# Requests for rows and weights, and steps of the last routing, placed between the outputs behind attention

## The chip, the cores and the metric

The kernel runs on one core of one Trainium2 chip. The metric is the device time of one execution in microseconds (us). The engines are named as in the profile: PE is TensorE (matrix products; PEld its weight loads), DVE is VectorE, ACT is ScalarE, POOL is GpSimd, SP is SyncE, which here only issues transfers.

## The reference

Two gated layers are applied to `x` of 4 sequences of 512 tokens with 256 features, in float32. Only the end of the second layer matters here, the feed-forward part with four experts:

```python
x = x + tanh(g_xattn[1]) * attention(layernorm(x), ctx)      # 16 heads, softmax
h = layernorm(x).reshape(-1, 256)
expert = argmax(h @ W_router, axis=-1)                       # one of 4 for each token
a = gelu(h @ W1[expert] + b1[expert])                        # 1024 wide, erf form
y = a @ Wo + bo + h
x = x + tanh(g_ffn[1]) * layer_norm(y, gamma, beta)
```

The reference computes all four experts for every token and keeps one.

## The kernel before

**Tiles by expert.** The kernel computes for each token only its own expert. Tokens are sorted into tiles of 128 of one expert each; 19 tiles (`T_ALL = 16 + 3`) are enough whatever the split. The lists are made in three goes (`LISTS`, `dispatch`): after two sequences tiles 0 to 4 are known, after three sequences tiles 5 to 8, and after the last sequence tiles 9 to 18. The last list needs the routing of the last sequence (`route(3)`), and that needs the last output of attention.

**What one tile needs.** `fetch_rows(j)` (L950) gathers 128 rows of 512 floats (the normed row, and the row to add the result to) by an indirect transfer from the scratch tensor `rows_d`, into a buffer `xr` (5 of them) or `xg`. `fetch_weights(j)` (L962) gathers the tile's first weight matrix with its bias, 128 x 2056 floats, into `wg`. Both are issued by POOL, on one queue with everything else that POOL does. `turn_tile(j)`, called t below, transposes the normed rows on PE (L974) and copies them on ACT (DVE for j = 4) to `xs` (L977). `hidden_half(j, f2)`, two of which make h, is 32 matrix products (L996) followed by GELU on ACT (L1009; for tiles 0 to 3 the GELU is deferred, since attention holds ACT's table). `output_tile(j)`, called o, is an addition on DVE (L1175), 16 matrix products `pyf` (L1178) and another addition on DVE (L1182). `norm_tile(j)` is the layer norm of the result: on DVE statistics (L1187, L1189) and variance (L1192), on POOL one power of -0.5 (L1193), and on DVE the rest (L1194, L1195 to L1200). L1194 doesn't need the power; L1195 does. `put_tile(j)` (L1205) writes the finished rows to the output by an indirect transfer that POOL issues; each such write waits for the one before it.

**The last routing.** `route(3)` consists of steps: `stats3` and `more3` (L325 to L340: layer norm statistics on DVE, power and correction on POOL), `norm3` (L360, L721: normed rows on DVE, then two writes to `rows_d` by SP, L725 and L726), `turn3` (8 transposes on PE, L371; the two halves of `xTf` are copied by ACT and by DVE, L372), `products3` (16 products `plT` with the router's weights on PE, L738, and a copy on ACT, L743), `logits3` (a transpose on PE, L748, and five small DVE steps, L751 to L756, that mark each token's expert in `onehot`), `ranks3` (two products `prk` on PE, L764, and sums on DVE, L767, L768). Then `dispatch(2)`: `lists`, `token_places` and `by_tile` (small DVE steps, L812 to L879; POOL clears one buffer, L872), `sels` (four selections of 128 x 512 on DVE, L899), `by_expert` (L886 to L892), `collected` (32 products `pidT` on PE, L912, and a copy on ACT, L917) and `tokens` (a transpose on PE, L921, and four small DVE steps, L923 to L930, that write the indices which `fetch_rows(9)` and later ones read).

**Order.** From here on no scheduler decides: each engine executes its instructions in the order in which the program emits them (`manual_schedule`). Behind the last attention group the program emits a block with all requests for tiles 5 to 8, into which the last routing's norm is put after the rows of tile 3, and then walks a list of items `queue`. For each item the loop emits the item; for an output it emits norm and put with it; then it emits the steps of the last routing that are assigned to this item (`steps`), and requests for later tiles. The order before is:

h4, o0, o1, o2, t5, o3, h5, t6, o4, h6, t7, o5, h7, t8, o6, h8, o7, t9, o8, h9, t10, h10, t11, o9, h11, and from there t, o, h for each tile.

The steps are assigned like this:

```python
    steps = {
        ("o", 1): [turn3], ("o", 2): [products3], ("o", 3): [logits3],
        ("h", 5): [ranks3, lists, token_places, by_tile], ("o", 4): [*sels, by_expert],
        ("o", 5): [collected], ("h", 7): [tokens],
    }
```

Requests for tiles 9 and 10 follow output 6, those for 11 follow output 7, and from output 8 on each output j is followed by those for tile j + 4. [...]

Of the kernel before, what the change touches and what calls it, by code (L numbers as in the profile page):

```python
# [20 lines left out]
B, S, D = 4, 512, 256  # L21
# [27 lines left out]
def flamingo_kernel(ctx: ExitStack, tc: tile.TileContext, t: dict, out: bass.AP):  # L49
    nc = tc.nc  # L50
# [654 lines left out]
    def route(b, eng=None):  # L705

        st = {}

        def stats():
            st["xn"] = act.tile([P, NT, D], F32, tag="xn", name=f"xn_f1_{b}")  # L710
            first, st["more"], st["rows"] = layernorm(
                x[b], st["xn"], 1e-5, f"f1_{b}", eng
            )
            first()

        def more_stats():
            st["more"]()

        def norm():
            st["rows"]()  # L720
            (eng or nc.gpsimd).tensor_tensor(  # L721
                x[b], x[b], bet1.unsqueeze(1).to_broadcast([P, NT, D]), ALU.add
            )
            rd = rows_d[b * S : (b + 1) * S, :].rearrange("(n p) d -> p n d", p=P)
            nc.sync.dma_start(out=rd[:, :, 0:D], in_=st["xn"])  # L725
            nc.sync.dma_start(out=rd[:, :, D : 2 * D], in_=x[b])  # L726

        def turn():
            st["xT"] = act.tile([P, NC, S], F32, tag="blocks", name=f"xTf1_{b}", bufs=1)
            transposed(st["xn"], st["xT"], f"f1_{b}")  # L730

        def products():


            plT = bank_psum(f"plT{b}")[:, 0:P]
            for c in range(NC):
                for n in range(NT):
                    nc.tensor.matmul(  # L738
                        plT[n * HP : (n + 1) * HP, :], lhsT=wr[:, c, :], rhs=st["xT"][:, c, ts(n, P)],
                        start=(c == 0), stop=(c == NC - 1),  # L740
                    )
            st["lT"] = const.tile([P, P], F32, tag="dec", name=f"lT{b}")
            nc.scalar.copy(st["lT"], plT)  # L743

        def logits():

            plg = bank_psum(f"plg{b}")[:, 0:P]
            nc.tensor.transpose(plg, st["lT"], ident)  # L748
            plg = plg.rearrange("p (n e) -> p n e", e=HP)[:, :, 0:NE]
            top = sml.tile([P, NT], F32, tag="top", name=f"top{b}")  # L750
            nc.vector.tensor_reduce(top, plg, AX.X, ALU.max)  # L751
            oh = onehot[:, ts(b, NT), :]
            nc.vector.tensor_tensor(oh, plg, top.unsqueeze(2).to_broadcast([P, NT, NE]), ALU.is_ge)
            nc.vector.tensor_tensor(oh, oh, order, ALU.mult)
            nc.vector.tensor_reduce(top, oh, AX.X, ALU.max)
            nc.vector.tensor_tensor(oh, oh, top.unsqueeze(2).to_broadcast([P, NT, NE]), ALU.is_equal)  # L756

        def ranks():
            prk = bank_psum(f"prk{b}")[:, 0 : 2 * NT * NE].rearrange(
                "p (i n e) -> p i n e", i=2, e=NE  # L760
            )
            oh = onehot[:, ts(b, NT), :]
            for i, m in enumerate((before, ones)):
                nc.tensor.matmul(prk[:, i], lhsT=m, rhs=oh, start=True, stop=True)  # L764
            for n in range(NT):
                k = b * NT + n
                nc.vector.tensor_tensor(count[:, k + 1, :], count[:, k, :], prk[:, 1, n, :], ALU.add)  # L767
            nc.vector.tensor_tensor(  # L768
                rank[:, ts(b, NT), :], prk[:, 0], count[:, b * NT : (b + 1) * NT, :], ALU.add
            )  # L770

        return [
            (stats, 0, 0), (more_stats, 0, 1), (norm, 0, 1), (turn, 0.9, 1), (products, 0.6, 1),
            (logits, 0.2, 1), (ranks, 0.5, 1),
        ]
# [167 lines left out]
    def fetch_rows(j):  # L943

        have = max(n for n, first in LISTS if first <= j or n == LISTS[0][0]) * S
        if j in (3, *range(LISTS[1][1], T_ALL)) and made["behind"]:
            xg[j] = act.tile([P, 2 * D], F32, tag="xr", name=f"xr{j}", bufs=5)
        else:
            xg[j] = wts.tile([P, 2 * D], F32, tag="xg", name=f"xg{j}", bufs=4)
        nc.gpsimd.indirect_dma_start(  # L950
            out=xg[j], out_offset=None, in_=rows_d[0:have, :],
            in_offset=bass.IndirectOffsetOnAxis(ap=get[:, j : j + 1], axis=0),
            bounds_check=have - 1, oob_is_err=False,
        )

    def fetch_weights(j):

        if j < T_AHEAD or (j - T_AHEAD) % 5 < 2:
            wg[j] = weight_place(f"wg{j}")
        else:  # L960
            wg[j] = act.tile([P, NC * FF + NF], F32, tag="wg", name=f"wg{j}", bufs=3)
        nc.gpsimd.indirect_dma_start(  # L962
            out=wg[j], out_offset=None, in_=t["w1e"],
            in_offset=bass.IndirectOffsetOnAxis(ap=wrow[:, j : j + 1], axis=0),
            bounds_check=NE * P - 1, oob_is_err=False,
        )
# [67 lines left out]
    for b in range(B):  # L1034
        first, rest = ffn0(b)
# [107 lines left out]
    for u in range(-NT, n_units):  # L1143
# [22 lines left out]
        if u in totals:  # L1166
            job, i = totals[u]
# [5 lines left out]
    def output_tile(j):  # L1173
        y = ys[j] = act.tile([P, D], F32, tag="y", name=f"y{j}", bufs=4)
        nc.vector.tensor_tensor(y, xg[j][:, 0:D], bo1, ALU.add)  # L1175
        py = bank_psum(f"pyf1_{j}")[:, 0:D]
        for f in range(NF):
            nc.tensor.matmul(  # L1178
                py, lhsT=hs[j, f // 4][:, f % 4, :], rhs=wo1[f // 4][:, f % 4, :],
                start=(f == 0), stop=(f == NF - 1),  # L1180
            )
        nc.vector.tensor_tensor(y, y, py, ALU.add)  # L1182

    def norm_tile(j):
        y = ys[j]
        st = sml.tile([P, 6], F32, tag="st", name=f"st_y{j}")
        nc.vector.bn_stats(st, y)  # L1187
        mv = sml.tile([P, NT, 2], F32, tag="mv", name=f"mv_y{j}")
        nc.vector.bn_aggr(mv[:, 0, :], st)  # L1189

        var, rstd, fix = (sml.tile([P, NT], F32, tag=v, name=f"{v}_y{j}") for v in ("var", "rstd", "fix"))
        nc.vector.tensor_scalar(var[:, 0:1], mv[:, 0, 1:2], 1e-12, None, ALU.add)  # L1192
        nc.gpsimd.tensor_tensor(rstd[:, 0:1], var[:, 0:1], power[:, 0:1], ALU.pow)  # L1193
        nc.vector.scalar_tensor_tensor(y, y, mv[:, 0, 0:1], gam1, ALU.subtract, ALU.mult)  # L1194
        nc.vector.scalar_tensor_tensor(  # L1195
            fix[:, 0:1], rstd[:, 0:1], var[:, 0:1], rstd[:, 0:1], ALU.mult, ALU.mult
        )
        nc.vector.tensor_scalar(fix[:, 0:1], fix[:, 0:1], -0.5, 1.5, ALU.mult, ALU.add)
        nc.vector.tensor_tensor(rstd[:, 0:1], rstd[:, 0:1], fix[:, 0:1], ALU.mult)
        nc.vector.scalar_tensor_tensor(  # L1200
            y, y, rstd[:, 0:1], xg[j][:, D : 2 * D], ALU.mult, ALU.add
        )
# [17 lines left out]
    att.__exit__(None, None, None)  # L1220
    act = ctx.enter_context(tc.tile_pool(name="moe", bufs=2))
    made["behind"] = True
    for j in (5, 3, 6, 7, 8):
        fetch_rows(j)
        if j > 3:
            fetch_weights(j)
        if j == 3:
            stats3, more3, norm3, turn3, products3, logits3, ranks3 = (
                job for job, *_ in route(B - 1, nc.vector)
            )  # L1230
            stats3()
            more3()
            norm3()
    lists, token_places, by_tile, *sels, by_expert, collected, tokens = (job for job, *_ in dispatch(2))


# [5 lines left out]
    first = LISTS[-1][1]  # L1242
    queue = [("h", 4), ("o", 0), ("o", 1), ("o", 2), ("t", 5), ("o", 3), ("h", 5)]
    for j in range(4, T_ALL - 2):
        queue += [("t", j + 2), ("o", j), ("h", j + 2)]
    for item, place in ((("o", first - 1), ("h", first)), (("t", first), ("o", first - 1))):
        queue.remove(item)
        queue.insert(queue.index(place), item)
    queue += [("o", T_ALL - 2), ("o", T_ALL - 1)]
    for kind, j in queue:  # L1250
        if kind == "h":
            for f2 in range(2):
                hidden_half(j, f2)
        elif kind == "t":
            turn_tile(j)
        else:
            if j < 3:
                for f2 in range(2):
                    activated(j + 1, f2)
            output_tile(j)  # L1260
            norm_tile(j)
            if j > 0:
                put_tile(j - 1)
        for job in steps.pop((kind, j), ()):
            job()
        for i in {("o", 6): (9, 10), ("o", 7): (11,)}.get((kind, j), ()):
            fetch_rows(i)
            fetch_weights(i)
        if kind == "o" and first <= j + 1 < T_ALL - 3:
            fetch_rows(j + 4)  # L1270
            fetch_weights(j + 4)
# [77 lines left out]
```

## Time and profile before

| | us |
|---|---|
| median of 3 runs | 862.4 |
| lowest and highest | 861.65 and 863.38 |
| profiled execution, its own time | 861.21 |
| its span, first to last instruction | 859.5 |
| PE busy | 821.1 (96%) |
| DVE busy | 561.7 (65%) |
| ACT busy | 422.5 (49%) |
| POOL busy | 277.4 (32%) |

The profile is one execution. An engine's busy time is the sum of its instructions in it, and an engine whose share is high in the mean can stand still in one stage. In the order of time each line has the start and the duration in us, the engine, the line of the kernel, output and input, and in square brackets how long the engine had stood idle and what ended that. A transfer that POOL issues (`DMA_INDIRECT`) shows there with the time that its issue took, not that of the transfer. The change lies between 710 and 785 us.

### The profile page before, as it was taken

To read this page: it belongs to the slowest core of one execution; us is meant where nothing else is said; L and a number is where in the kernel's file an instruction comes from. 1 tells how busy PE (TensorE), PEld (TensorE's weight loads), DVE (VectorE), ACT (ScalarE), POOL (GpSimd) and SP (SyncE) were. 2 spreads that over 40 slices of the span, in tenths; PEclk is the share of its full clock that TensorE was granted. 3 is DMA by queue.
4 is the path that set the end of the run, shared out by engine and by line. 5 is a ranking of instruction groups with operands and counts; after the bars stand their busy time and mean duration, and the time that the engine had idled before them with its cause. 6 is when DMAs were issued, how large, how long until landed. Compare 5 with 4: busy or idle time off the path is not lost. (4 is left out here: it accounts for less than half of the span.)

```text
span 859.5 us, 13597 instructions
## 1 busy us (share of the span) xinstructions
PE 821.1 (96%) x5241; PEld 462.1 (54%) x5241; DVE 561.7 (65%) x1218; ACT 422.5 (49%) x886; POOL 277.4 (32%) x446
## 2 busy tenths in 40 slices
PE   6999999999999999999999999999999996999994
PEld 3444454445464346445554445634545655888993
DVE  6878778766857784768646865577877645753443
ACT  2576475553555452655435563357556564223331
POOL 5536365424342422311100120012033216244542
PEclk9999999999999999999999999999999998899998
DMA  8100000000000000000000010001032328136540
GB/s 312 64 1 1 1 2 2 1 1 0 2 13 25 1 1 0 26 0 2 1 1 25 1 50 1 1 1 50 1 119 96 106 75 292 40 93 233 195 155 14
DMA packets 18096, 43.07 MB, mean 50 GB/s; under 512 B 2222, under 2 KB 12208, under 8 KB 15600
## 3 DMA queue, kind: packets, MB, share of 16 engines
q0 software_dynamic: 5488, 28.13, 9.6%
q1 hardware_dynamic: 12128, 13.54, 4.7%
q8 instruction: 41, 0.67, 0.3%
q10 hardware_dynamic: 416, 0.54, 0.2%
q14 instruction: 23, 0.19, 0.1%
HBM read 35.91 MB, written 6.68 MB: 50 GB/s over the span
## 5 line engine op out<-in xcount | busy, mean ns | idle before, releaser
L508 DVE TENSOR_REDUCE m<-pm 128x1 f32<-128x512 f32 x512 | 316.9, 682 | 107.6 <-PE psc L494 105.2
L523 ACT ACTIVATE p<-psc 128x512 f32<-128x512 f32 x512 | 267.1, 602 | 150.9 <-PE psc L494 148.3
L494 PE MATMUL psc<-q,k 32*128 32x512 f32 x1024 | 279.5, 622 | 0.2 <-DVE h L672 0.2
L494 PE MATMUL pm<-k,q 32*128 32x512 f32 x1024 | 262.1, 615 | 1.3 <-ACT q L481 0.9
L526 POOL TENSOR_TENSOR p<-p,dec 128x256 f32<-128x256 f32 x128 | 93.6, 735 | 177.2 <-ACT p L523 177.2
L494 PEld LDWEIGHTS pm<-k,q 32*128 32x128 f32 x1024 | 92.7, 184 | 83.5 <-issue 50.0
L494 PEld LDWEIGHTS psc<-q,k 32*128 32x128 f32 x1024 | 106.6, 183 | 52.2 <-issue 25.7
L551 PE MATMUL po<-p,v 128*32 128x512 f32 x1024 | 116.5, 595 | 1.9 <-DVE m L508 1.9
L551 PEld LDWEIGHTS po<-p,v 128*32 128x32 f32 x1024 | 31.7, 109 | 81.8 <-issue 60.8
L996 PE MATMUL pg<-xs,wg 128*128 128x128 f32 x608 | 72.4, 276 | 1.8 <-ACT xs L977 1.3
L996 PEld LDWEIGHTS pg<-xs,wg 128*128 128x128 f32 x608 | 70.5, 192 | 5.9 <-issue 1.7
L1178 PE MATMUL pyf<-wo,ha 128*128 128x256 f32 x304 | 70.3, 387 | 0.0
L1009 ACT ACTIVATE ha<-pg,wg 128x128 f32<-128x128 f32 x120 | 34.2, 368 | 69.6 <-PE pg L996 66.8
L619 POOL TENSOR_TENSOR x<-x,o 128x256 f32<-128x256 f32 x14 | 10.2, 729 | 174.4 <-DVE o L612 131.7
L1178 PEld LDWEIGHTS pyf<-wo,ha 128*128 128x128 f32 x304 | 57.9, 195 | 7.5
L664 PE MATMUL ph<-xTf,w1q 128*128 128x512 f32 x128 | 60.0, 605 | 0.0
L379 PE MATMUL py_f<-w2q,h 128*128 128x256 f32 x256 | 57.2, 381 | 0.0
L557 ACT COPY oT<-po 128x512 f32<-128x512 f32 x32 | 18.7, 584 | 77.6 <-PE po L551 77.6
L379 PEld LDWEIGHTS py_f<-w2q,h 128*128 128x128 f32 x256 | 48.0, 190 | 9.4 <-DVE m L508 3.0
L451 PE MATMUL pk<-cT,wk 128*128 128x512 f32 x68 | 35.3, 644 | 7.2 <-DMA cT<-in_ctxT_dram 7.2
L1182 DVE TENSOR_TENSOR y<-y,pyf 128x256 f32<-128x256 f32 x19 | 8.0, 421 | 47.4 <-PE pyf L1178 43.4
L664 PEld LDWEIGHTS ph<-xTf,w1q 128*128 128x128 f32 x128 | 22.6, 189 | 30.4 <-issue 18.2
(223 smaller groups left out, 810.1 us busy)
## 6 DMA issues: line engine op xcount, KB each, us to landing
x<-in_x_dram SPq DMA_DIRECT2D x4, 512.0 KB, 7.0
rows_d<-xn_f SPq DMA_DIRECT2D x4, 512.0 KB, 3.0
rows_d<-x SPq DMA_DIRECT2D x4, 512.0 KB, 3.1
cT<-in_ctxT_dram SPq DMA_DIRECT2D x3, 512.0 KB, 9.5
w1q<-in_w_dram SPq DMA_DIRECT2D x1, 1024.0 KB
w2q<-in_w_dram SPq DMA_DIRECT2D x1, 1024.0 KB, 11.3
wo<-in_wo_dram SPq DMA_DIRECT2D x2, 512.0 KB
rows<-in_rows_dram SPq DMA_DIRECT2D x1, 640.0 KB, 9.2
```

Source lines behind the costliest of these rows:

```text
L379: nc.tensor.matmul(py[:, n, :], lhsT=operand(c, n0 + n), rhs=w[:, c, :], start=(c == 0), stop=(c == chunks - 1),)
L451: nc.tensor.matmul(pp, lhsT=attn_w[layer][w][:, c, ts(tt, P)], rhs=src[:, c, :], start=(c == 0), stop=(c == NC - 1),)
L494: nc.tensor.matmul(out_, lhsT=lhs[r, ts(n, P)], rhs=rhs[r, :], start=True, stop=True)
L508: nc.vector.tensor_reduce(m[:, n, 2 * pair + i, r : r + 1], pm[i], AX.X, ALU.max)
L523: nc.scalar.activation(p[:, i, :], psc[i], AF.Exp, scale=SCALE)
L526: nc.gpsimd.tensor_tensor(d, d, dec.unsqueeze(1).to_broadcast([P, 2, P]), ALU.mult)
L551: nc.tensor.matmul(po[i * HP : (i + 1) * HP, :], lhsT=v_sb[b % 2][0][:, kt, c0 : c0 + HP], rhs=ps_exp[NT * s + kt, i // 2][:, i % 2, :], s ...
L557: nc.scalar.copy(pos[s], po)
L664: nc.tensor.matmul(ph, lhsT=w1q[:, c, ts(f, P)], rhs=st["xT"][:, c, :], start=(c == 0), stop=(c == NC - 1),)
L996: nc.tensor.matmul(ph[:, f, :], lhsT=w[:, c, ts(f2 * NF // 2 + f, P)], rhs=xs[j][:, c, :], start=(c == 0), stop=(c == NC - 1),)
L1009: nc.scalar.activation(ha[:, f, :], (ha if src is None else src)[:, f, :], AF.Gelu, bias=biases[j][:, fa : fa + 1],)
L1178: nc.tensor.matmul(py, lhsT=hs[j, f // 4][:, f % 4, :], rhs=wo1[f // 4][:, f % 4, :], start=(f == 0), stop=(f == NF - 1),)
```

## The change

It touches only the part behind attention, and only the order.

1. Of the requests that stood in one block, rows and weights of tile 5 and rows of tile 3 stay there, and so does the norm of the last routing. Rows and weights of tile 6 now follow hidden 4, those of tile 7 follow output 0 with its norm, those of tile 8 follow output 1 with its norm and the put of tile 0.
2. The steps of the last routing that are assigned to an output now come between the output and its norm: `turn3` ahead of norm 1, `products3` ahead of norm 2, `logits3` ahead of norm 3, `sels` and `by_expert` ahead of norm 4, `collected` ahead of norm 5. Steps assigned to a hidden stay behind it.
3. In the list of items, t10 comes before h9: o7, t9, o8, t10, h9, h10, t11.

```diff
     made["behind"] = True
-    for j in (5, 3, 6, 7, 8):
-        fetch_rows(j)
-        if j > 3:
-            fetch_weights(j)
-        if j == 3:
-            stats3, more3, norm3, turn3, products3, logits3, ranks3 = (
-                job for job, *_ in route(B - 1, nc.vector)
-            )
-            stats3()
-            more3()
-            norm3()
+    fetch_rows(5)
+    fetch_weights(5)
+    fetch_rows(3)
+    stats3, more3, norm3, turn3, products3, logits3, ranks3 = (job for job, *_ in route(B - 1, nc.vector))
+    stats3()
+    more3()
+    norm3()
@@
-    for item, place in ((("o", first - 1), ("h", first)), (("t", first), ("o", first - 1))):
+    for item, place in (
+        (("o", first - 1), ("h", first)), (("t", first), ("o", first - 1)),
+        (("t", first + 1), ("h", first)),
+    ):
         queue.remove(item)
         queue.insert(queue.index(place), item)
@@
             output_tile(j)
+        for job in steps.pop((kind, j), ()):
+            job()
+        if kind == "o":
             norm_tile(j)
             if j > 0:
                 put_tile(j - 1)
-        for job in steps.pop((kind, j), ()):
-            job()
-        for i in {("o", 6): (9, 10), ("o", 7): (11,)}.get((kind, j), ()):
+        fetches = {("h", 4): (6,), ("o", 0): (7,), ("o", 1): (8,), ("o", 6): (9, 10), ("o", 7): (11,)}
+        for i in fetches.get((kind, j), ()):
             fetch_rows(i)
             fetch_weights(i)
```

## The prediction

> **What bounds the kernel now.** I read the page's 40 slices first, for a place where TensorE (PE) is not full, then PE's own waits from 700 us on, then each engine in order of time around the longest of them.
>
> ```profile
> PE   6999999999999999999999999999999996999994
> PEclk9999999999999999999999999999999998899998
> ```
>
> PE is full except at both ends and in the slice that begins at 33 x 21.5 = 709 us; the clock digits fall there too. PE's waits in 700 to 860 us (line, releaser: total, times, longest):
>
> ```profile
> PE plT L738 <- DVE xTf L372: 8.3, 1, 8.3
> PE pg L996 <- ACT xs L977: 1.3, 1, 1.3
> PE prk L764 <- DVE onehot L756: 0.7, 1, 0.7
> ...
> PE pg L996 <- DMA wg<-in_w1e_dram,wrow: 0.2, 1, 0.2
> ```
>
> One wait holds most of it: the router product plT waits for the second half of the transposed rows xTf, which VectorE (DVE) copies out of PSUM. The copy's input was on PE at 717.42 and its pair on ScalarE (ACT) was done at 718.65. The order in time on PE, DVE and GpSimd (POOL) shows why it came late:
>
> ```profile
> 717.42 1.04 PE L371 MATMUL pt_f<-ident,xn_f 128*128 128x128 f32 x8
> ...
> 730.56 0.66 PE L738 MATMUL plT<-xTf,wr 128*32 128x128 f32 x8 [8.29 <-DVE xTf L372]
> 731.14 0.69 PE L974 MATMUL ptx<-ident,xr 128*128 128x128 f32 x2
> 731.62 5.54 PE L1178 MATMUL pyf<-wo,ha 128*128 128x256 f32 x16
> ```
> ```profile
> 720.00 0.47 DVE L1194 SCALAR_TENSOR_TENSOR y<-y,mv_y,rows 128x256 f32<-128x256 f32 x1
> 725.09 0.22 DVE L1195 SCALAR_TENSOR_TENSOR fix_y<-rstd_y,var_y 128x1 f32<-128x1 f32 x1 [4.61 <-POOL rstd_y L1193]
> ...
> 729.82 0.68 DVE L372 COPY xTf<-pt_f 128x512 f32<-128x512 f32 x1
> ```
> ```profile
> 716.19 1.29 POOL L950 DMA_INDIRECT xr<-rows_d,get  x1 [0.51 <-issue]
> 717.79 1.44 POOL L962 DMA_INDIRECT wg<-in_w1e_dram,wrow  x1 [0.30 <-issue]
> 719.53 1.00 POOL L950 DMA_INDIRECT xr<-rows_d,get  x1 [0.30 <-issue]
> ...
> 724.47 0.59 POOL L1193 TENSOR_TENSOR rstd_y<-var_y,power 128x1 f32<-128x1 f32 x1
> ```
>
> DVE's copy stands behind the norms of tiles 0 and 1; norm 0 stops for its power on POOL; and that power stands behind six requests (rows and weights of tiles 6, 7, 8), ready at 720.08 but started at 724.47. The clock in stretches (us, PE, PEld, DVE, ACT, POOL, clock, DMA):
>
> ```profile
> 722.30:725.20 2.90, 0.00 (x0) 0.00 (x0) 0.11 (x1) 0.00 (x0) 2.43 (x3) 1.00 1.02 395
> 725.20:730.50 5.30, 0.00 (x0) 0.00 (x0) 4.44 (x16) 0.00 (x0) 1.78 (x2) 0.50 1.03 431
> 730.60:735.50 4.90, 4.90 (x20) 3.71 (x21) 3.17 (x11) 0.64 (x2) 1.76 (x2) 0.50 0.28 112
> ```
>
> The clock halves 2.9 us into the idle time and stays halved for 4.9 us of work: the wait has a tail.
>
> **What the Trainium skill says.** "TensorE: Matmul & The Clock Gate", Part 1: an idle window of about 3.4 us halves PE's clock, about 3.4 us of work restores it, and the window runs freely. The trace agrees within the freedom of the window (2.9 and 4.9 us); the idle 1.27 us before 778.12 left the clock full. The same page's table calls the queues of DVE, ACT and POOL strict FIFO, which is the trap seen above. "SBUF — State Buffer", SBUF: two separate sides: a DVE operation in a two-port mode keeps POOL from writing the descriptors of a request. Requests 6 took 1.29 and 1.44 us beside the DVE work of 715.72 to 718.35, the later ones 1.00. "DMA: Bandwidth & Descriptors", Anatomy of one DMA: 2.0 us plus bytes/436e3. For a weight tile (128 x 2056 x 4 = 1.05 MB) I estimate 4.4 us from it; weights 9, issued by 767.67, released PE at 772.82, 5.1 us later with rows 9 ahead of them. The trace decides.
>
> **The change, part by part.** No instruction is added or removed; order moves on all engines but SP.
>
> *Requests 7 and 8 behind the powers of norms 0 and 1.* Requests 6 stay and end at 719.23, ahead of the power's input. Norm 0's sum is at 718.80 on DVE. The undisturbed norm (at 726.65 to 729.82) sets offsets from that sum: variance ready +1.28, power +1.37 to +2.10, L1195 +2.13, next instruction +3.17, next sum +3.69. So power 0 runs 720.17 to 720.89 and the sum of tile 1 starts at 722.49 (before: 726.65).
>
> *The turn ahead of norm 1.* The copy follows that sum by 0.45 at 722.94 instead of 729.82. Before, plT started 0.74 after the copy: now 723.68, not 730.56. PE stops at 722.27 either way, so the gap is 1.41 instead of 8.29: **-6.88 us**.
>
> *Clock.* With 1.41 us the gap stays below 2.9, so the clock should hold. The same three steps at full clock have pitches on PE of 0.38, 0.25 and 3.45 (twins at 721.85, 741.97 and 742.22) against 0.58, 0.48 and 5.38: **-2.36 us**.
>
> *Logits ahead of norm 3, but later on DVE.* After the copy: norm 1's variance 724.38; POOL has issued rows and weights 7 by 720.89 + 2 x 1.30 = 723.5, so power 1 ends at 725.2 and the sum of tile 2 is at 726.8, variance 728.1. POOL meanwhile issues output 0 (1.25) and rows and weights 8 (2.60), until 729.05: power 2 is now the late one, by 1 us, and ends at 729.65. Sum of tile 3: 731.2. Logits: five steps, 1.15 us until prk can start: 731.66 + 1.15 = 732.81. PE, from 723.68 by the pitches (0.38, 0.25, 3.45, 0.11, 3.74), is there at 731.61: a wait of 1.20 in place of 0.68, **+0.52 us**. Sum at prk: 741.53 - 732.81 = 8.72 saved. PE does not wait for power 3, which runs at 733.6 and is free of the queue.
>
> *Selections ahead of norm 4.* Norm 3 now stands between the logits and the counts, so the counts start at 732.66 + 2.7 = 735.4; counts to row list 4.88, tile 4's two additions 0.97, four selections 2.49: done at 743.7. PE needs them 11.48 after prk (753.01 - 741.53): 744.3. It fits with 0.6 to spare; unmoved, norm 4 would have stood in between with 3.2 us. Norms 4 and 5 then end at 750.7, the tokens follow by 751.4; PE sends them at 749.0. Rows 9 are requested at 765.31 - 8.72 = 756.6, after norm 6 in both kernels: 5 us of cover. *Collected ahead of norm 5*: it has no DVE or POOL step; zero.
>
> *Moved past.* Rows and weights 6 are issued where they were; 7 end at 723.5 (before 721.8), 8 at 729.05 (before 724.4). Their transfers then end some 5 us later at most, near 736 by the 731 seen, while PE turns tile 7 at about 740 and tile 8 at 749: zero, by that cover. SP's two writes of rows (717.30, 718.38) stay and are read first by rows 9. Output 1 waits for output 0, now between the weights; bounded below as a rival.
>
> *Tile 10's turn ahead of hidden 9.* In the old times: PE was free of output 8 at 772.64, waited 0.18 for weights 9, and 1.27 for xs10, whose copy stood on ACT behind hidden 9's activations. Now the copy is early, but PE must first have rows 10, queued behind weights 9. Landing X is not shown. From the bytes moved (209 GB/s at 765.4 and so on, summed to 131 + 262 + 1053 + 262 KB of output, rows, weights, rows) I estimate 772.9 plus a completion, 773.5; bounds 772.7 and 774.8. Hidden 10 would start at X + 0.25 + 3.57 = 777.3, but not before weights 10, estimated at 777.2, against 778.12: **-0.7 us**, bounds -0.9 and +0.5. I take -0.6.
>
> Sum: -6.88 - 2.36 + 0.52 - 0.6 = -9.3. From 785 us on PE repeats 7.24 us per tile without a wait; nothing there gives it back. The profiled execution took 861.21 (span 859.5 and 1.71 around it), 1.19 below the median of 862.4 and under the lowest of the three. 861.21 - 9.3 = 851.9; with the same offset the median is **853.1**.
>
> **Rivals.** *The clock falls anyway.* The window runs freely and two short gaps (1.41 and 1.20) lie 9 us apart; for it, nothing but the freedom of the window; against it, the 1.27 us gap. The 2.36 comes back: 855.5. *Tile 10's turn becomes the wait.* If rows 10 land only with weights 10, at about 776.9, PE stands 4.3 us and cools: hidden 10 at 780.7, plus 2.4, is 5.0 late in place of 0.6 early: 862.4 - 8.7 + 5.0 = 858.7. Against it: rows 9 released PE within 2.4 us of their issue. *POOL gets a new wait that ends slower.* Output 1 must wait for output 0's landing, which now stands behind weights 7, and power 3 is queued behind output 1. Output 0 is issued by 726.5; the longest landing seen is output 6's, 772.12 to 777.28, 5.2 us, which gives 731.7 against power 3's 733.6. It decides from the point where power 3 is late by 0.6 + 9.3 + 1.7: a landing after about 744. At 20 us it costs 746.5 + 1.4 - 733.6 - 0.6 = 13.7, so 862.4 - 9.3 + 13.7 = 866.8. *It doesn't do what it says:* the orders of the built programs show the moves on each engine, so only a wait that the profile of before hides would leave 862.
>
> **How the numbers follow.** Forecast 0.78, clock 0.11, tile 10 0.05, output wait 0.04, nothing 0.02. A measurement of this kernel tells about 0.2% (1.7 us) from no change. Faster: 0.78 + 0.11 + 0.05 = 0.94; same 0.02; slower 0.04. The range must hold 8 in 10: the forecast's own terms (tile 10 within -0.3 and +1.1, DVE's chain within 1 us) span 851.8 to 855.0; stretched to 855.8 it takes in the clock rival.
>
> **What would show it.** Right: plT's wait near 1.4 at 722 to 724, powers of L1193 starting about 0.1 after their variances at tiles 0 and 1 and a wait of about 1 us at tile 2, clock 1.00 throughout, the output product L1178 at 3.6 and not 5.5, prk's wait near 1.2, no wait for xs10 at hidden 10. Wrong: a stall at the product of the selections (L912), PE waiting for xr at tile 10 over 2 us, POOL's L1205 waiting on its own DMA near 731, or weights 7 or 8 named as a releaser.

## The result, and the profile after

| | before | after |
|---|---|---|
| median of 4 runs each, us | 862.22 | 853.12 |
| lowest to highest | 861.65 to 863.38 | 852.40 to 853.87 |
| profiled execution, own time | 861.21 | 852.66 |
| its span | 859.5 | 851.0 |
| from the first L371 of the last routing to the end of the last L1178 | 129.41 | 120.54 |

The ratio after to before is 0.9893, with a 95% interval of 0.9876 to 0.9910: 9.1 us less, where 853.1 was predicted. The last row of the table, called the **stage** below, is worked out from each profile: the start of the first of the routing's transposes (717.42 before, 717.78 after), taken from the end of the last product (846.83 and 838.32). It leaves out all that lies ahead of the change, which differs from run to run. The stage became 8.87 us shorter.

The page's slices of after, PE and its clock:

```profile
PE   6999999999999999999999999999999999999994
PEclk9999999999999999999999999999999999999998
```

The dip of PE in slice 33 is gone, and with it that of the clock in slices 33 and 34. PE's waits from 700 to 860 us (line, releaser: total, times, longest):

```profile
PE ptx L974 <- DMA xr<-rows_d,get: 1.4, 1, 1.4
PE prk L764 <- DVE onehot L756: 1.4, 1, 1.4
PE plT L738 <- DVE xTf L372: 1.3, 1, 1.3
...
```

The wait of 8.3 us of plT has become 1.3. The wait of hidden 10 for xs10 is gone, that of tile 10's turn for its rows (ptx) is new, and prk waits twice as long as before. POOL in the order of time:

```profile
720.53 0.74 POOL L1193 TENSOR_TENSOR rstd_y<-var_y,power 128x1 f32<-128x1 f32 x1 [0.94 <-DVE var_y L1192]
721.47 1.06 POOL L950 DMA_INDIRECT xr<-rows_d,get  x1 [0.19 <-issue]
...
724.72 0.74 POOL L1193 TENSOR_TENSOR rstd_y<-var_y,power 128x1 f32<-128x1 f32 x1 [0.89 <-DVE var_y L1192]
725.65 1.05 POOL L1205 DMA_INDIRECT out_dram<-y,put  x1 [0.20 <-issue]
...
728.36 1.25 POOL L962 DMA_INDIRECT wg<-in_w1e_dram,wrow  x1 [0.31 <-issue]
729.63 0.58 POOL L1193 TENSOR_TENSOR rstd_y<-var_y,power 128x1 f32<-128x1 f32 x1
732.32 1.05 POOL L1205 DMA_INDIRECT out_dram<-y,put  x1 [2.11 <-DMA out_dram<-y,put]
734.04 0.66 POOL L1193 TENSOR_TENSOR rstd_y<-var_y,power 128x1 f32<-128x1 f32 x1 [0.67 <-DVE var_y L1192]
```

Powers 0, 1 and 3 wait for their variance and start as soon as it is there. Power 2 has no bracket: POOL came to it straight from the issue of weights 8, and DVE was waiting. DVE at the copy and at norm 2, and PE from the copy on and at tile 10:

```profile
723.21 0.68 DVE L372 COPY xTf<-pt_f 128x512 f32<-128x512 f32 x1
...
730.25 0.22 DVE L1195 SCALAR_TENSOR_TENSOR fix_y<-rstd_y,var_y 128x1 f32<-128x1 f32 x1 [1.52 <-POOL rstd_y L1193]
```
```profile
723.95 0.42 PE L738 MATMUL plT<-xTf,wr 128*32 128x128 f32 x8 [1.32 <-DVE xTf L372]
724.30 0.44 PE L974 MATMUL ptx<-ident,xr 128*128 128x128 f32 x2
724.58 3.62 PE L1178 MATMUL pyf<-wo,ha 128*128 128x256 f32 x16
...
733.29 0.37 PE L764 MATMUL prk<-onehot,before 128*128 128x16 f32 x2 [1.41 <-DVE onehot L756]
...
765.86 0.44 PE L974 MATMUL ptx<-ident,xr 128*128 128x128 f32 x2 [1.45 <-DMA xr<-rows_d,get]
```

Output product 3 takes 3.62 us and not 5.54: the clock held.

### The profile page after: what moved, and what is told of

Read it like the earlier page. It is cut to its first block, busy times and chain, and to the rows that moved or that the text cites. A ratio compares the mean times of both kernels' runs of the same rounds, so it can differ in the third digit from the quotient of the medians.

```text
span 851.0 us, 13599 instructions
## 1 busy us (share of the span) xinstructions
PE 818.3 (96%) x5241; PEld 460.4 (54%) x5241; DVE 561.3 (66%) x1218; ACT 422.5 (50%) x886; POOL 277.8 (33%) x446
## 5 line engine op out<-in xcount | busy, mean ns | idle before, releaser
L1178 PE MATMUL pyf<-wo,ha 128*128 128x256 f32 x304 | 68.4, 379 | 0.0
L1178 PEld LDWEIGHTS pyf<-wo,ha 128*128 128x128 f32 x304 | 56.4, 190 | 7.0
```

What stands on the lines that cost most here:

```text
L1178: nc.tensor.matmul(py, lhsT=hs[j, f // 4][:, f % 4, :], rhs=wo1[f // 4][:, f % 4, :], start=(f == 0), stop=(f == NF - 1),)
```

## The experiments

The theory: the gain is the idle time of plT, which has two causes in series (on POOL the power behind the requests, on DVE the copy behind two norms), and the halved clock behind that idle time, which goes only when the idle time is short. Of the six requests ahead of power 0, the last four delay it: those for tile 6 had been issued by 719.23, before its input was ready at 720.08. Rivals: one of the two causes is all of it, or the slow products have another reason. Runs came in three groups; each group has its own runs of before, and the times of one group are compared with those.

| kernel | median us | before in its group | ratio, 95% interval | stage us |
|---|---|---|---|---|
| e1_requests | 859.41 | 862.54 | 0.9960 (0.9946 to 0.9974) | 125.97 |
| e2_steps | 858.59 | 862.54 | 0.9963 (0.9947 to 0.9979) | 125.61 |
| e3_turn10 | 862.99 | 862.54 | 1.0003 (0.9994 to 1.0012) | 128.87 |
| e4_filler | 866.67 | 862.54 | 1.0056 (1.0039 to 1.0072) | 133.50 |
| a_parts12 | 853.66 | 863.50 | 0.9892 (0.9878 to 0.9907) | 120.93 |
| a_rows10 | 853.71 | 863.50 | 0.9898 (0.9883 to 0.9913) | 120.98 |
| a_late8 | 853.11 | 863.50 | 0.9885 (0.9871 to 0.9899) | 119.82 |
| a_best | 851.82 | 863.50 | 0.9871 (0.9857 to 0.9885) | 119.27 |
| after_ref | 852.13 | 861.30 | 0.9889 (0.9874 to 0.9905) | 119.87 |
| e5_filler32 | 858.81 | 861.30 | 0.9972 (0.9960 to 0.9984) | 127.36 |
| a_early9 | 848.86 | 861.30 | 0.9860 (0.9845 to 0.9875) | 117.00 |
| a_early9_logits | 848.74 | 861.30 | 0.9853 (0.9838 to 0.9868) | 116.14 |

### Each part alone

**e1_requests**: only the requests move, on before: the block becomes rows and weights 5 and rows 3 with the last routing's norm, and the list behind the items becomes

```diff
-        for i in {("o", 6): (9, 10), ("o", 7): (11,)}.get((kind, j), ()):
+        fetches = {("h", 4): (6,), ("o", 0): (7,), ("o", 1): (8,), ("o", 6): (9, 10), ("o", 7): (11,)}
+        for i in fetches.get((kind, j), ()):
```

> Part 1 alone: the requests for tiles 6, 7 and 8 between the items; the steps of the last routing stay behind the norms, tile 10's turn behind hidden 9. Theory (power behind six requests, then the copy behind two norms): in the times of before, power 0 ends at 720.9, the sum of tile 1 is at 722.5, but the copy xTf still waits for the whole norm 1 and comes at 725.7, so plT restarts at 726.4 after a gap of 4.1 us. That is over 2.9 us, so the clock still halves; prk comes at about 737.3 instead of 741.5. About 858.0 us, 4.2 below before; down to 855.7 if the clock comes back sooner. Rival (all of the gain is the power's queue): 853 to 854. Rival (all of the gain is the order on VectorE): 862.

**e2_steps**: the move of the steps, on before.

```diff
             output_tile(j)
+        for job in steps.pop((kind, j), ()):
+            job()
+        if kind == "o":
             norm_tile(j)
             if j > 0:
                 put_tile(j - 1)
-        for job in steps.pop((kind, j), ()):
-            job()
```

> Part 2 alone: the steps of the last routing ahead of the norms; the six requests stay in one block ahead of power 0, tile 10's turn stays behind hidden 9. Theory: power 0 is late as in before (724.5), the sum of tile 1 at 726.65, the copy at 727.0, plT at 727.7: a gap of 5.5 us, the clock halves, prk is ready about when hidden 5 ends, at 738.0 instead of 741.5. About 858.7 us, 3.5 below before. The separate gains of parts 1 and 2 (4.2 and 3.5) then do not reach the 9 of both, because each alone leaves the gap above 2.9 us and the clock's 2.4 us unsaved. Rival (order on VectorE is all of it): 853 to 854. Rival (the queue on GpSimd is all of it): 862.

PE at plT and output 3, first of e1_requests, then of e2_steps:

```profile
728.46 0.66 PE L738 MATMUL plT<-xTf,wr 128*32 128x128 f32 x8 [4.17 <-DVE xTf L372]
729.05 0.69 PE L974 MATMUL ptx<-ident,xr 128*128 128x128 f32 x2
729.53 6.05 PE L1178 MATMUL pyf<-wo,ha 128*128 128x256 f32 x16
```
```profile
728.74 0.65 PE L738 MATMUL plT<-xTf,wr 128*32 128x128 f32 x8 [5.49 <-DVE xTf L372]
729.32 0.69 PE L974 MATMUL ptx<-ident,xr 128*128 128x128 f32 x2
729.80 5.05 PE L1178 MATMUL pyf<-wo,ha 128*128 128x256 f32 x16
```

The gaps are those expected (4.1 and 5.5 us), and the products behind them are still slow. Neither cause alone is the gain: 3.1 and 4.0 us by the medians, 3.44 and 3.80 us of stage, together 7.24, where both at once (a_parts12) give 8.48. The idle times at plT do add up: 4.12 and 2.80 us less alone, 6.98 with both. What goes only with both is the clock. It is worth more than the 1.24 us that the sum lacks, because prk waits 1.4 us with both causes gone, 0.7 in e1_requests and not at all in e2_steps. Prk came 3.60 and 4.14 us earlier than in before, counted from the first transpose, where 4.2 and 3.5 were expected: from plT to the logits' transpose PE needs 4.08 us at full clock, 6.96 in e1_requests, 5.95 in e2_steps and 6.44 in before. The halved clock thus cost 2.9, 1.9 and 2.4 us behind gaps of 4.2, 5.5 and 8.3 us; it does not grow with the gap. The longer and the shorter tail also account for most of what the two expectations missed at prk.

**e3_turn10**: t10 ahead of h9, on before. **a_parts12**: the changed kernel without that. The line between them:

```diff
+        (("t", first + 1), ("h", first)),
```

> Part 3 alone: tile 10's turn ahead of hidden 9. Theory: the wait of 1.27 us for xs10 goes and a wait of about 1.4 us for rows 10 comes, with hidden 10 some 0.3 us earlier: 861.9 us, not to be told from before. Rival (the turn's wait costs as much as the prediction's tile 10 case): slower by up to 2 us.

> The changed kernel without part 3 (tile 10's turn behind hidden 9 as before). Theory: parts 1 and 2 carry the change; part 3 was worth 0.3 us by the trace, so about 853.4 us. Rival (part 3 is worth the 0.6 predicted, or costs time since the turn now waits 1.45 us for rows 10): 853.7, or 852.

Part 3 alone can't be told from nothing by time. The stages give it 0.54 us on before (0.17 of it because output 3 was slowed less in that trace) and 0.39 us on parts 1 and 2: a small gain, within what differs from run to run (after_ref repeats after with a stage shorter by 0.67, its wait for rows 10 being 0.8 in place of 1.4).

### The clock by itself

**e4_filler** and **e5_filler32** put products that nobody reads between the two halves of plT, on before; 64 and 32 of them:

```diff
             for c in range(NC):
+                if b == B - 1 and c == 1:
+                    fill = bank_psum("fill")[:, 0:P]
+                    for _ in range(32):
+                        nc.tensor.matmul(fill, lhsT=ident, rhs=ident, start=True, stop=True)
                 for n in range(NT):
```

> Before, with 64 matrix products of the identity by itself, read by nobody, on TensorE between the two halves of the last router product plT, so that TensorE works through 7 of the 8.3 us for which it waits. Nothing else moves; the copy xTf comes as late as in before. Theory (the slow products behind the gap are the halved clock): the clock stays full, the output product of tile 3 takes 3.6 instead of 5.5 us, and the time falls by 2.4 us to 859.9. Rival (those products are slow for another reason, such as the transfers in flight): 862.2 or more.

> As the filler kernel, with 32 products in place of 64: each turned out to be two passes of 0.113 us, so 64 of them lasted 14.6 us and overran the wait of 8.3 us by 6.2. 32 last 7.3 us and end before the copy xTf. Theory (halved clock behind the gap): output product 3 at 3.6 us, 2.4 us less than before: 859.9. Rival (the products are slow because of the weight transfers in flight, which the longer filler had outlasted): 862.2, output product 3 still at 5.5 us.

The first overran the wait, since each of the products takes two passes of PE (128 records for 64 products); it lost 4.1 us and tells of the clock only that output product 3 took 3.62 us. The second fits. PE of e5_filler32:

```profile
723.00 7.41 PE L740 MATMUL fill<-ident 128*128 128x128 f32 x64
731.41 0.43 PE L742 MATMUL plT<-xTf,wr 128*32 128x128 f32 x8 [0.99 <-DVE xTf L372]
731.76 0.44 PE L978 MATMUL ptx<-ident,xr 128*128 128x128 f32 x2
732.04 3.62 PE L1182 MATMUL pyf<-wo,ha 128*128 128x256 f32 x16
```

The copy is as late as in before (plT's second half starts 13.18 us after the first transpose, 13.14 in before), the weight transfers are the same, and useless work on PE makes the kernel faster by 2.5 us (median). Prk comes 2.41 us earlier from the first transpose; the stage is 2.05 us shorter, since hidden 9 then waits 0.3 us longer for its weights. The term of 2.36 us in the prediction is thus the clock. The rival, transfers in flight, fails in before too: there the DMA engines moved 0 GB/s from 732.5 to 734.5, while output product 3 ran at a clock of 0.50.

When the clock fell and came back, in the four traces in which it did so at plT, gives a reason for the uneven cost (the cost is what the steps from plT to the logits' transpose took above 4.08 us):

| trace | idle time at plT, us | clock halved, us into it | time at 0.50, us | part of that behind the gap, us | cost, us |
|---|---|---|---|---|---|
| before | 8.29 | 2.98 | 10.24 | 4.93 | 2.36 |
| e3_turn10 | 8.28 | 2.65 | 10.24 | 4.61 | 2.19 |
| e1_requests | 4.17 | 3.34 | 6.83 | 6.00 | 2.88 |
| e2_steps | 5.49 | 2.61 | 6.83 | 3.95 | 1.87 |

The time at half clock was two or three times 3.41 us. The switches of a whole trace lie on such a grid: in e1_requests the clock halved at 727.63, was full again at 734.46, and halved at the end of the kernel at 850.51, 2 and 36 steps later. In all four traces the full clock came back at the end of the step that followed the one in which PE had resumed, and the cost was 0.47 to 0.48 of the part behind the gap. So the tail depended on where in a step PE resumed, and not on the length of the gap. From these four I estimate that it can cost between 1.6 us (one step) and 3.3 us (two). The 2.9 us of the prediction is therefore the reading of one trace and no threshold: the four show 2.6 to 3.3. Gaps of up to 1.78 us (a_late8, tile 10) left the clock full, and no run here has a gap between that and 4.17.

### What is left, and a faster version

**a_rows10** requests rows 10 ahead of weights 9, on the changed kernel:

```diff
         for i in fetches.get((kind, j), ()):
             fetch_rows(i)
+        for i in fetches.get((kind, j), ()):
             fetch_weights(i)
```

> The changed kernel with rows 10 requested ahead of weights 9 (rows 9, rows 10, weights 9, weights 10). Theory (one queue, served in order: rows 10 land late because 1.05 MB of weights 9 is ahead of them): TensorE's wait of 1.45 us for rows 10 goes, a shorter one for weights 9 comes, since they land 0.65 to 1.3 us later; 0.2 to 0.9 us less, 852.5. Rival (the rows' landing is a fixed latency behind their issue): the wait shrinks only by the 1.3 us of the earlier issue and weights 9 take its place in full: 853.1.

A miss: the rival's outcome came, with weights 9 taking the wait over in full. PE at hidden 9 and hidden 10:

```profile
766.73 3.81 PE L996 MATMUL pg<-xs,wg 128*128 128x128 f32 x32 [1.50 <-DMA wg<-in_w1e_dram,wrow]
770.79 3.81 PE L996 MATMUL pg<-xs,wg 128*128 128x128 f32 x32 [0.25 <-DMA wg<-in_w1e_dram,wrow]
```

Rows 10 are there in time, but hidden 9 starts 48.25 us after the first transpose (48.36 in after): weights 9 now come as late as rows 10 did, and weights 10 are late too. Changing the order in the group of transfers gained nothing; that the group as a whole is requested too late is what the next runs try.

**a_late8** moves rows and weights 8 in the list of requests:

```diff
-... ("o", 0): (7,), ("o", 1): (8,), ("o", 6): (9, 10), ...
+... ("o", 0): (7,), ("h", 5): (8,), ("o", 6): (9, 10), ...
```

**a_best** joins it with a_rows10 and copies both halves of the last xTf on ACT:

```diff
-            transposed(st["xn"], st["xT"], f"f1_{b}")
+            transposed(st["xn"], st["xT"], f"f1_{b}", b == B - 1)
```

> The changed kernel with rows and weights 8 requested behind hidden 5 and its steps instead of behind output 1. Theory: power 2 no longer stands behind them, starts 0.1 us after its variance, the logits come 1.05 us earlier and TensorE's wait at prk falls from 1.4 to about 0.4: 852.05 us. Rival (GpSimd stops at output 1, which waits for output 0's landing, and power 3 behind it is then late): the gain at prk is lost again at the product of the selections, 853 to 854.

> The changed kernel with three edits: requests 8 behind hidden 5, rows 10 ahead of weights 9, and both halves of the last xTf copied by ScalarE, which is idle there. Theory: plT no longer waits for VectorE (1.3 us of wait to none), the chain on VectorE is 0.6 us shorter, prk then waits about 1.1 us; together 1.65 at prk and 0.6 at tile 10: 850.8 us. Rival (prk is set by the chain of norms on VectorE alone and ScalarE's second copy delays the activations of tile 3): 852.

PE's waits at prk and tile 10 in a_late8, and POOL at output 1 and power 3 there:

```profile
PE ptx L974 <- DMA xr<-rows_d,get: 1.8, 1, 1.8
...
PE prk L764 <- DVE onehot L756: 0.3, 1, 0.3
```
```profile
732.05 1.04 POOL L1205 DMA_INDIRECT out_dram<-y,put  x1 [2.61 <-DMA out_dram<-y,put]
733.27 0.66 POOL L1193 TENSOR_TENSOR rstd_y<-var_y,power 128x1 f32<-128x1 f32 x1 [0.18 <-DVE var_y L1192]
```

Prk is 1.08 us earlier, as worked out, and power 3 just clears output 1: between them POOL is idle for 0.18 us, until the variance is there. But PE, coming earlier, waits 0.33 us longer for rows 10, and 0.72 us of stage remain; by the times it can't be told from the changed kernel (853.11, where 852.05 was expected). In a_best prk is 1.64 us earlier (1.65 expected), plT has no wait, and the 0.6 us at tile 10 did not come, as in a_rows10. Its time of 851.82 is accordingly nearer to the rival's 852 than to the 850.8 expected.

**a_early9** therefore requests tile 9 earlier: a_late8's edit, both halves on ACT, and

```diff
-        fetches = {("h", 4): (6,), ("o", 0): (7,), ("o", 1): (8,), ("o", 6): (9, 10), ("o", 7): (11,)}
+        fetches = {("h", 4): (6,), ("o", 0): (7,), ("h", 5): (8,), ("h", 7): (9,), ("o", 6): (10,), ("o", 7): (11,)}
```

> The changed kernel with requests 8 behind hidden 5, both halves of the last xTf on ScalarE, and rows and weights 9 requested right behind the tokens (after hidden 7) instead of after output 6, where rows and weights 10 stay. Theory (tiles 9 and 10 wait because four transfers, 2.6 MB, are asked for within 5 us, though the indices of tile 9 are there 5 us before its request): no wait on transfers is left at tiles 9 and 10 (1.45 us in the changed kernel, 1.78 with late requests 8), prk's wait stays near 1.3 us; about 117.5 us from the first transpose of the routing to the last product, 850.1 us. Rival (the request behind hidden 7 holds up power 6 or finds no free buffer, so that tile 9 gains nothing): 851.8.

> The changed kernel unaltered, as the measure for the others of this group: 853.1 us; from the first of the routing's transposes to the last output product 120.5 us, against 129.4 before.

**a_early9_logits** moves the logits besides:

```diff
-        ("o", 1): [turn3], ("o", 2): [products3], ("o", 3): [logits3],
+        ("o", 1): [turn3], ("o", 2): [products3], ("t", 5): [logits3],
```

> The same, and the logits placed behind tile 5's turn instead of behind output 3, so that VectorE marks the experts ahead of tile 3's two additions. Theory: the logits come 1.0 us earlier and prk's wait falls from 1.3 to 0.3 us, but the selections are not earlier, and TensorE catches up with them after 0.65 us: 0.65 us less than without it, 849.5. Rival (TensorE now stops at the logits' transpose for ScalarE's copy and gains nothing): 850.1 or more.

POOL at the request of rows 9 in a_early9, then PE's waits behind attention in a_early9 and in a_early9_logits:

```profile
750.01 1.27 POOL L950 DMA_INDIRECT xr<-rows_d,get  x1 [0.49 <-DVE put L930]
```
```profile
PE prk L764 <- DVE onehot L756: 1.3, 1, 1.3
```
```profile
PE prk L764 <- DVE onehot L756: 0.2, 1, 0.2
```

Rows 9 are issued as soon as the tokens are written, and no wait for a transfer is left. Against a_best, which shares its two other edits but has rows 10 requested first instead, the stage of a_early9 is 2.27 us shorter. Since rows 10 first cost 0.44 us of stage in a_rows10, I estimate that the earlier request brings 1.8 to 2.3 us. Stage 117.00 (117.5 expected) and 116.14: the logits gave 0.86 where 0.65 was expected, and PE did not stop at the selections. Against the changed kernel in the same group (852.13) the two run 3.3 and 3.4 us faster. Between them the times don't decide; only the traces do, one of each.

## Why the prediction was right

Times of after are told here less 0.36 us, by which its first transpose was later than in before.

- **Requests behind the powers.** Power 0 was predicted at 720.17 and ran at 720.17; the sum of tile 1 followed at 722.51, predicted 722.49.
- **The turn ahead of norm 1.** The copy came 0.34 us after that sum and not 0.45, plT at 723.59 (predicted 723.68), the gap was 1.32 (1.41). The term -6.88 measured -6.97.
- **Clock.** Full throughout; plT to the logits' transpose 4.08, as its twins said. The term -2.36 is confirmed apart by e5_filler32 (-2.41 at prk). The first rival, that the clock falls anyway, did not happen. The reason given, a gap under 2.9 us, was no threshold (see the table above), and the size of the term belongs to the one trace of before: in e3_turn10 the same idle time cost 2.19.
- **Logits.** Power 2 is the late one, as predicted, but by 1.3 in place of 1.0 us: weights 8 took 1.25 us to issue, not 1.00. DVE worked beside it for only its first 0.4 us, so what lengthened it is not shown, and neither is it for requests 6. Prk came at 732.93 (732.81) and waited 1.41 (1.20): the term +0.52 measured +0.73. a_late8 shows the cause: with requests 8 out of its way, prk comes 1.08 us earlier.
- **Selections.** Done at 743.6 (743.7 predicted), asked for at 744.4: the cover held with 0.8 us. Tokens at 751.45 (751.4), rows 9 requested at 756.7 (756.6).
- **Tile 10.** The least certain term. Rows 10 let PE go on at 774.1 in the times of before (8.24 us later than the 765.86 of after), where 773.5 was estimated between 772.7 and 774.8; so the gain was 0.3 us and not the 0.6 taken. The estimate put 0.6 us between the last bytes (772.9) and the landing, where 1.2 us would have been right; whether the completion or the 772.9 was off, no run shows.
- **The output's wait.** The prediction named POOL waiting for its own output near 731 as a sign of being wrong. The wait is there, until 731.96 (predicted 731.7), and did no harm: power 3 needed POOL only 1.7 us later, 0.7 us after output 1 was issued. The rival's mechanism is real, and its price was far under its point of decision.

Sum of the terms as measured: -6.97 - 2.36 + 0.73 - 0.3 = -8.9, the stage's -8.87. The sum of the prediction was -9.3. The profiled execution fell by 8.55, since its part ahead of the change was 0.36 us longer; the medians fell by 9.1. That the median came within 0.1 us of the forecast is partly luck: the medians of one kernel differ by 1 to 2 us from group to group (852.13 and 853.12 for after, 861.30 to 863.50 for before).

## What to carry to other kernels

A small operation on an engine that also issues transfers waits for all issues ahead of it (here power 0, for 4.4 us); look at what another engine's queue holds behind that operation before placing a block of requests there. When two waits stand in series, removing one may bring less than its share, because the idle time's tail (here the halved clock) went only when the whole idle time was short (1.3 us, not 4.2 or 5.5). When PE has been moved forward, the next bound can be a transfer that was on time before (here rows 10): ask for it when its indices are ready, not when its old place in the order comes.

## What the runs showed of the hardware

- Halved clock: the tail cost 2.9, 1.9, 2.4 and 2.2 us behind gaps of 4.2, 5.5, 8.3 and 8.3 us, and nothing behind gaps of 1.3 to 1.8 us. In each trace the clock switched on a grid of 3.41 us, and its place in a step, not the gap, went with the cost.
- A float32 product of 128 x 128 with 128 columns appears as two records, 0.113 us apart at full clock (e4_filler: 64 products, 128 records, 14.49 us until the next product starts).
- The time from the end of an output's issue (131 KB) until the next output, which waits for it, could start went with the weights requested shortly before it: 5.2 us in before (outputs 6 and 7), 5.6 in after (0 and 1), 6.7 in a_rows10 (6 and 7), but 2.0 in a_late8 and 1.9 in a_early9 (1 and 2), where the last request for weights lay more than 8 us back.
- The same instructions ahead of the change brought the first transpose to 717.03 us in one profile and to 719.92 in another. A spread of that size lies ahead of the stage, so the stage in a trace can tell apart what the times do not. Two traces of one kernel still differ in it: by 0.67 us in after and after_ref, nearly all of it the wait for rows 10 (1.45 and 0.83).
